# Softmax quotient of a dynamic convolution: sum in its own tile, limit on GpSimd, reciprocal in two separated halves

## The chip, the cores and the metric

The kernel runs on one core of a Trainium2 chip. All times are device microseconds of that core, from one launch. In profile lines PE is TensorE (PEld its weight loads), DVE is VectorE, ACT is ScalarE, POOL is GpSimd and SP is SyncE, which here only issues DMAs; a q behind a name is the engine's sequencer.

## The reference

The input is 8 images of 256 channels and 64 x 64 points, float32 throughout. Two residual layers follow each other. Layer 0 adds an involution: per point, 9 weights per group of 8 channels come out of a small network of 1 x 1 convolutions, and weigh a 3 x 3 neighbourhood. Layer 1 adds a local 7 x 7 attention and a dynamic convolution. The diff touches the second half of the dynamic convolution and the scaled weights of layer 0. Cut down to those:

```python
def _gn(v, G=32, eps=1e-5):                      # mean and variance of groups of 8 channels
    ...
    return ((g - m) / jnp.sqrt(s + eps)).reshape(v.shape)

x = x + _L0_conv_ref(_gn(x), ...)                # layer 0: x1, x2, x3 are 1x1 convolutions of _gn(x)
x = x + _L1_conv_ref(_gn(x), ...)                # layer 1

# inside layer 1, on y = _gn(x)
wts = jnp.einsum('oc,bchw->bohw', Wfc, y).reshape(b, C, 9, h, w)
wts = jax.nn.softmax(wts, axis=2)                # over the 9 branches of each channel
xr = jnp.broadcast_to(y[:, None], (b, 9, c, h, w)).reshape(b * 9, c, h, w)
hid = jax.nn.relu(_dwconv(xr, w1))
oc = _dwconv(hid, w2).reshape(b, 9, C, h, w)
out_conv = jnp.sum(oc * wts.transpose(0, 2, 1, 3, 4), axis=1)
return rate1 * out_att + rate2 * out_conv
```

The nine branches of `oc` are equal, so the kernel computes one depthwise result and multiplies it by the sum of the nine softmax weights, written out as a quotient. The middle branch's weights `Wfc` are subtracted from the other eight at the start, so that its exponential is 1. With T the sum of the eight other exponentials and S = min(1 + T, 1e37), the factor is S times the reciprocal of S.

## The kernel before, in words

**Tiling.** An image is cut into 8 bands of 8 rows; a band of one tile of 128 channels is 128 x 512 numbers. There are two channel tiles (`ct` 0 and 1). Layer 1 works through the 64 bands in order (`g` counts them), and a band takes 8 steps: four for `ct` 0 (`m` 0 to 3, steps 0 to 3) and four for `ct` 1 (steps 4 to 7). Layer 0 runs 12 bands ahead (`AHEAD`) and is woven into the same steps, so that the last image's layer 1 has no layer 0 beside it.

**A step of layer 1.** TensorE computes the attention's weighted values of an earlier step (L747) and the scores of this one (L703) into one PSUM tile `sco`. DVE masks the scores and takes their maximum (L712) and adds the weighted values to `xr` (L757). TensorE transposes the previous step's probabilities (L735). ACT takes the exponentials (L720), DVE the small reciprocal of their sums (L727, 128 x 2), ACT scales them (L729). Beside that, TensorE computes two of the eight branch products `pf` (L825, two matmuls each of them), ACT writes their exponentials into `ex` (L830, a tile of 128 x 2 x 512, three buffers), and POOL adds the tile of the step before into this one (L1026). DVE adds depthwise taps (L782, L808). One more group of matmuls may stand in the middle of a step: queries (L637), keys (L658), values (L563, L607).

**The order.** The kernel writes out each engine's order by hand. `after(n, f)` puts `f` at n places from now; `advance()` moves on by one place and runs what has come due. A step has six places: after the scores and L757; after the first `pf`; after L729; after the middle group; after the second `pf`; at the step's end. Every engine executes its instructions in the order in which this one program issued them.

**The quotient.** After a channel tile's last step, `dynamic_sum` comes four places later. It lets POOL add the two halves of the last `ex` tile (L838) into the second half. Five places later, at the next step's first place, DVE adds 1 and limits the sum (L845, `tensor_scalar`) and takes the reciprocal of the first half (L846, 256 columns); three places later it takes the other half's (L850); two places later POOL multiplies (L855), multiplies `oc` (L856) and adds into `xr` (L857). After the second channel tile, six places later, SP stores `xr` (L862). For the very last tile of the launch, DVE does POOL's part.

**Scaled weights.** Once per image, `scaled_weights` multiplies layer 0's weights by the group norm's factor, per input channel: L296 (128 x 64) and L297 (128 x 256), twice each, on DVE. The factor comes from `gn_affine`, whose last part takes a small reciprocal on DVE (L266).

**Layer 0's part in a step.** L328 and L369 are its 1 x 1 convolutions, L429 and L447 the small network, L460 (DVE) the product of the nine weights with shifted values into `prod` (two buffers), and L468 (POOL) adds `prod` into `xg`. The adds of one band stand in the order of its nine products.

Of the kernel before, what the change touches and what calls it, by code (L numbers as in the profile page):

```python
# [10 lines left out]
F32 = mybir.dt.float32  # L11
BF16 = mybir.dt.bfloat16
AF = mybir.ActivationFunctionType
ALU = mybir.AluOpType
# [4 lines left out]
P = 128  # L19
C = 256  # L20
NCT = C // P
# [3 lines left out]
BAND = R * W  # L25
# [61 lines left out]
def conv_layers_kernel(ctx: ExitStack, tc: tile.TileContext, ins: dict, out: bass.AP):  # L87
    nc = tc.nc
# [18 lines left out]
    def load(name, shape, src=None, now=True):  # L107
        t = const.tile(shape, F32, name=f"c_{name}")
        late.append(lambda: nc.scalar.dma_start(out=t, in_=ins[name] if src is None else src))
        if now:  # L110
            late.pop()()
        return t
# [5 lines left out]
    w12 = load("w12", [P, NCT, 2 * REL], ins["w12"].rearrange("(t p) n -> p t n", p=P))  # L118
    w3 = load("w3", [P, NCT, C], ins["w3"].rearrange("(t p) n -> p t n", p=P))
# [62 lines left out]
    w1 = ctx.enter_context(tc.tile_pool(name="l1", bufs=2))  # L182
# [3 lines left out]
    def layer1_loads():  # L186


        last = w1.tile([P, NCT, 1, C], F32, tag="rec", name="last", bufs=1)
        for f in late:  # L190
            f()
        nc.scalar.dma_start(out=last, in_=wfc_in[:, :, KK - 1 :])

        def first():
            nc.vector.tensor_scalar(wv, wv, rate1, None, ALU.mult)

        def difference(kt):
            nc.vector.tensor_sub(wfc[:, kt], wfc[:, kt], last[:, kt].to_broadcast([P, KK - 1, C]))  # L200

        return [first, lambda: difference(0), lambda: difference(1)]
# [12 lines left out]
    def after(n, f):  # L215
        later.append((place[0] + n, f))
# [8 lines left out]
    def gn_affine(sts, means, name, done):  # L225


        n = len(sts)
        mv = stat.tile([P, n, 2], F32, name=f"mv_{name}", tag=f"mv{n}")
        for ct, st in enumerate(sts):  # L230
            nc.vector.bn_aggr(mv[:, ct, :], st)
        mean, var = mv[:, :, 0], mv[:, :, 1]
        gm, d, sc, bi = (stat.tile([P, n], F32, name=f"{v}_{name}", tag=f"{v}{n}") for v in ("gm", "d", "sc", "bi"))

        def group_means(v, k):
            pg = ps.tile([P, n], F32, name=f"pg_{name}_{k}", tag="gen", bufs=5)
            nc.tensor.matmul(pg, means, v, start=True, stop=True)
            return pg


        def a1():
            pg = group_means(mean, 0)
            after(2, lambda: a2(pg))

        def a2(pg):
            nc.vector.tensor_copy(gm, pg)
            for ct in range(n):
                c = slice(ct, ct + 1)
                nc.vector.tensor_scalar(d[:, c], pg[:, c], mean[:, c], None, ALU.subtract)
                nc.vector.tensor_scalar(d[:, c], d[:, c], d[:, c], var[:, c], ALU.mult, ALU.add)  # L250
            after(5, a3)

        def a3():
            pg = group_means(d, 1)
            after(2, lambda: a4(pg))

        def a4(pg):
            nc.vector.tensor_scalar(sc, pg, GN_EPS, None, ALU.add)
            after(2, a5)

        def a5():
            nc.scalar.activation(sc, sc, AF.Sqrt)
            after(4, a6)

        def a6():
            nc.vector.reciprocal(sc, sc)  # L266
            for ct in range(n):
                c = slice(ct, ct + 1)
                nc.vector.tensor_scalar(bi[:, c], gm[:, c], sc[:, c], -1.0, ALU.mult, ALU.mult)
            done(sc, bi)  # L270

        after(3, a1)
# [15 lines left out]
    def scaled_weights(b):  # L288

        im = images[b]  # L290

        def scale(sc, bi):
            im.w12s = w0.tile([P, NCT, 2 * REL], F32, tag="w12s", name=f"w12s_{b}", bufs=1)
            im.w3s = w0.tile([P, NCT, C], F32, tag="w3s", name=f"w3s_{b}", bufs=1)
            for kt in range(NCT):
                nc.vector.tensor_scalar(im.w12s[:, kt], w12[:, kt], sc[:, kt : kt + 1], None, ALU.mult)  # L296
                nc.vector.tensor_scalar(im.w3s[:, kt], w3[:, kt], sc[:, kt : kt + 1], None, ALU.mult)  # L297
            after(5, lambda: through(bi))

        def through(bi):  # L300
            pb = ps.tile([P, 1 + NCT], F32, tag="gen", name=f"pb_{b}", bufs=5)
            for m, to, w in ((0, 0, w12), (0, 64, w12), (1, 0, w3[:, :, :P]), (2, 0, w3[:, :, P:])):
                for kt in range(NCT):
                    nc.tensor.matmul(
                        pb[to : to + w.shape[2], m : m + 1], w[:, kt], bi[:, kt : kt + 1],
                        start=(kt == 0), stop=(kt == NCT - 1),
                    )
            after(2, lambda: biases(pb))

        def biases(pb):  # L310
            im.bias = w0.tile([P, 1 + NCT], F32, tag="bias", name=f"bias_{b}")
            nc.vector.tensor_add(im.bias[:, 0:1], pb[:, 0:1], par[:, PB21 : PB21 + 1])
            for ct in range(NCT):
                nc.vector.tensor_add(
                    im.bias[:, 1 + ct : 2 + ct], pb[:, 1 + ct : 2 + ct], chan[:, ct, CB3 : CB3 + 1]
                )

        gn_affine([im.st0[:, ct] for ct in range(NCT)], gmat, f"a{b}", scale)

    def small_maps(b, i):  # L320
# [396 lines left out]
    def exponentials(nm, prob, nmax):  # L717
        tot = w1.tile([P, 2], F32, tag="tot", name=f"tot_{nm}", bufs=4)
        for h in range(2):
            nc.scalar.activation(  # L720
                prob[:, h, :NKEY], prob[:, h, :NKEY], AF.Exp, bias=nmax[:, h : h + 1], scale=-1.0,
                accum_out=tot[:, h : h + 1],
            )
        return tot
# [90 lines left out]
    def depthwise_end(b, i, ct, acc):  # L815

        oc = w1.tile([P, BAND], F32, tag="oc", name=f"oc_{b}_{i}_{ct}")
        nc.scalar.activation(oc, acc.rearrange("p r c -> p (r c)"), AF.Copy, scale=rate2)
        return oc
# [11 lines left out]

    def dynamic_sum(b, i, ct, ex, oc):

        tot = ex[:, 1]
        xr = images[b].xr[i]

        engine = nc.vector if (b, i, ct) == (B - 1, NB - 1, NCT - 1) else nc.gpsimd
        engine.tensor_add(tot, tot, ex[:, 0])  # L838
        rec = w1.tile([P, BAND], F32, tag="rec", name=f"rec_{b}_{i}_{ct}", bufs=1)
        n = BAND // 2  # L840

        def quotient():


            nc.vector.tensor_scalar(tot, tot, 1.0, 1.0e37, ALU.add, ALU.min)  # L845
            nc.vector.reciprocal(rec[:, :n], tot[:, :n])  # L846
            after(3, second)

        def second():
            nc.vector.reciprocal(rec[:, n:], tot[:, n:])  # L850
            after(2, weigh)

        def weigh():

            engine.tensor_mul(tot, tot, rec)  # L855
            engine.tensor_mul(oc, oc, tot)  # L856
            engine.tensor_add(xr[:, ct], xr[:, ct], oc)  # L857
            if ct == NCT - 1:
                after(6, store)

        def store():
            nc.sync.dma_start(  # L862
                out=out[b].rearrange("(t p) n -> p t n", p=P)[:, :, i * BAND : (i + 1) * BAND], in_=xr
            )

        after(5, quotient)


    def beside(g, s):
# [93 lines left out]
    with tc.manual_schedule():  # L963
# [17 lines left out]
        for n, f in enumerate(layer1_loads()):  # L981
            after(4 * STEPS * (3 + n), f)

        pending, before, conv = [], None, None
        for g in range(-AHEAD, B * NB):
            b, i = divmod(g, NB)
            for s in range(STEPS):
                ct, m = divmod(s, NT // 2)
                mid, end = beside(g, s)
                steer(g, s)  # L990
                if g >= 0:
# [9 lines left out]
                    tot = exponentials(nm, prob, nmax)  # L1001
                advance()
                if g >= 0:
                    ex, exb = w1.tile([P, 2, BAND], F32, tag="ex", name=f"ex_{nm}", bufs=3), ex if m else None
# [18 lines left out]
                if g >= 0:  # L1023
                    branch_weights(b, i, ct, m, 1, ex)
                    if exb is not None:
                        after(4, lambda ex=ex, exb=exb: nc.gpsimd.tensor_add(ex, ex, exb))  # L1026
                    if m == 1:
                        conv[1]()
                        conv = depthwise_middle(b, i, ct)
                    if m == NT // 2 - 1:  # L1030
                        oc = depthwise_end(b, i, ct, conv[1])
                        after(4, lambda a=(b, i, ct, ex, oc): dynamic_sum(*a))
# [97 lines left out]
```

## Time and profile before

| | |
|---|---|
| median of 3 runs | 4155.27 us (4154.16 to 4160.41) |
| the profiled execution | 4152.64 us |
| its span, first to last instruction | 4150.9 us |
| mean granted TensorE clock | 0.993 |
| busy PE, PEld | 4022.6 us (97%), 2126.8 us (51%) |
| busy DVE, ACT, POOL | 3591.9 us (87%), 3081.0 us (74%), 2923.0 us (70%) |
| L845 on DVE | 128 times, 136.9 us, and 33.0 us idle ahead of it |
| L846, L850 on DVE | 128 times each, 224.4 us and 223.5 us |
| L838, L855, L856, L857 on POOL | 127 times each, 161.5 to 162.3 us each |
| L296 and L297 on DVE | 16 times each, 15.9 us and 17.0 us |

A group's line gives, behind its shapes and its count, the busy time and the mean of one in ns, and then the idle time of the engine just before it with what ended that. Matmuls overlap in the records, so a PE that reads 97% busy can hide gaps of a tenth of a microsecond; a step's length against the matmuls in it shows them. The chain is followed back from the last instruction, from each to what released it.

### The profile page before, as it was taken

Reading aid. Unit: us, or ns where it says so; the run is one execution under the profiler, and the core shown is the slowest. Engines: PE = TensorE matmul, PEld = TensorE weight load, DVE = VectorE, ACT = ScalarE, POOL = GpSimd, SP = SyncE. Lnnn points to the kernel's source line nnn. Section 1 sums busy time; section 2 is a strip of 40 time slices with the busy share of each in tenths; the row PEclk is TensorE's granted clock in tenths of the full one; section 3 lists DMA queues with packets and bytes.
Section 4 is the critical chain, followed back from the end, with each engine's and each line's share of the span. In section 5 each row is a group of like instructions: output and inputs, shape, how many; then the busy total and the mean of one; then the engine's idle time right before and its main releaser. Section 6 shows DMA issues by size and latency. Waiting matters only on the chain.

```text
span 4150.9 us, 72735 instructions
## 1 busy us (share of the span) xinstructions
PE 4022.6 (97%) x25292; PEld 2126.8 (51%) x25292; DVE 3591.9 (87%) x7248; ACT 3081.0 (74%) x7726; POOL 2923.0 (70%) x1902
## 2 busy tenths in 40 slices
PE   6789999999999999999999999999999999999998
PEld 3345555555555555555555555555555555455554
DVE  5878998899898898889998898888988889977777
ACT  3467778777787777877778777777778777687776
POOL 4767777677786777777777777777777677744554
PEclk8999999999999999999999999999999999999999
DMA  8854234234244233334234234244233233111100
GB/s 226 194 135 111 73 91 109 72 94 109 62 101 107 76 94 98 81 94 109 72 85 118 72 94 105 66 101 106 71 82 99 65 87 85 33 41 39 39 28 21
DMA packets 381264, 367.89 MB, mean 89 GB/s; under 512 B 55648, under 2 KB 282720, under 8 KB 380640
## 3 DMA queue, kind: packets, MB, share of 16 engines
q1 hardware_dynamic: 377568, 358.68, 34.3%
q8 instruction: 200, 3.28, 0.3%
q10 hardware_dynamic: 3328, 4.55, 0.3%
q14 instruction: 168, 1.38, 0.1%
HBM read 261.42 MB, written 101.71 MB: 87 GB/s over the span
## 4 chain that ended last, share of the span: by engine, by line
PE 71%; DVE 14%; POOL 6%; ACT 5%; DMA 2%; issue 2%; SPq 1%; POOLq 0%; ACTq 0%; DVEq 0%
PE pf L825 33%; PE ptp L735 5%; PE sco L747 5%; PE pk L658 5%; PE sco L703 5%; PE p L369 5%; DVE prod L460 4%; PE pq L637 4%; POOL xg L468 3%; PE pvt L607 2%; PE pv L563 2%; DVE acc L808 2%; PE pw L447 2%; DVE acc L782 2%; POOL ex L1026 2%
## 5 line engine op out<-in xcount | busy, mean ns | idle before, releaser
L825 PE MATMUL pf<-yp,c_wfc 128*128 128x512 f32 x4096 | 1930.5, 595 | 10.6 <-ACT vc L581 5.0
L468 POOL TENSOR_TENSOR xg<-xg,prod 128x1024 f32<-128x1024 f32 x549 | 1203.9, 2193 | 96.6 <-DVE prod L460 64.1
L825 PEld LDWEIGHTS pf<-yp,c_wfc 128*128 128x128 f32 x4096 | 729.9, 190 | 690.5 <-issue 619.4
L1026 POOL TENSOR_TENSOR ex<-ex,ex 128x1024 f32<-128x1024 f32 x384 | 907.7, 2364 | 61.9 <-ACT ex L830 57.2
L830 ACT ACTIVATE ex<-pf 128x512 f32<-128x512 f32 x1024 | 607.3, 593 | 297.9 <-POOL ex L1026 141.3
L782 DVE SCALAR_TENSOR_TENSOR acc<-yp,c_chan,acc 128x504 f32<-128x504 f32 (+3 forms) x1104 | 766.2, 694 | 42.3 <-ACT acc L773 21.7
L460 DVE SCALAR_TENSOR_TENSOR prod<-pw,c_par,x3q 128x1040 f32<-128x1040 f32 x576 | 733.9, 1281 | 66.8 <-PE pw L447 21.6
L808 DVE SCALAR_TENSOR_TENSOR acc<-hid,c_chan,acc 128x504 f32<-128x504 f32 (+3 forms) x1024 | 757.8, 740 | 20.2 <-ACT acc L802 2.1
L855 POOL TENSOR_TENSOR ex<-ex,rec 128x512 f32<-128x512 f32 x127 | 162.3, 1278 | 809.5 <-DVE rec L850 767.1
L729 ACT ACTIVATE prob<-prob,tot 128x196 f32<-128x196 f32 x1024 | 411.6, 450 | 387.2 <-DVE tot L727 386.4
L712 DVE CUSTOM_DVE_ANT_0 prob<-sco,c_mask 128x196 f32<-128x196 f32 x1024 | 325.5, 355 | 272.4 <-PE sco L703 272.0
L720 ACT ACTIVATE prob<-prob,nmax 128x196 f32<-128x196 f32 x1024 | 461.4, 454 | 46.9 <-DVE nmax L712 45.3
L747 PEld LDWEIGHTS sco<-pt,vt 112*64 112x64 f32 x8160 | 283.8, 137 | 182.3 <-issue 51.7
L737 ACT COPY pt<-ptp 112x512 f32<-112x512 f32 x511 | 297.0, 581 | 105.0 <-PE ptp L735 103.0
L735 PE MATMUL ptp<-ident,prob 128*112 128x128 f32 x2044 | 341.7, 287 | 31.2 <-ACT prob L729 30.5
L747 PE MATMUL sco<-pt,vt 112*64 112x64 f32 x8160 | 347.0, 227 | 0.0
L735 PEld LDWEIGHTS ptp<-ident,prob 128*112 128x112 f32 x2044 | 203.9, 133 | 201.4 <-issue 77.7
L703 PE MATMUL sco<-kb,qb 64*64 64x196 f32 x4096 | 295.2, 357 | 0.0
L563 PE MATMUL pv<-yp,c_wv 128*128 128x512 f32 (+2 forms) x576 | 247.3, 554 | 0.6
L369 PE MATMUL p<-xc,w3s 128*128 128x512 f32 x512 | 244.4, 601 | 0.0
L658 PE MATMUL pk<-yp,c_wk 128*128 128x512 f32 (+2 forms) x576 | 240.8, 545 | 0.0
L637 PE MATMUL pq<-yp,c_wq 128*128 128x512 f32 x512 | 240.6, 592 | 0.0
(140 smaller groups left out, 5294.0 us busy)
## 6 DMA issues: line engine op xcount, KB each, us to landing
x<-x3n SPq DMA_DIRECT2D x128, 264.0 KB, 2.1
x3q<-x SPq DMA_DIRECT2D x128, 264.0 KB, 7.2
xc<-in_x SPq DMA_DIRECT2D x64, 512.0 KB, 5.0
xg<-in_x SPq DMA_DIRECT2D x256, 128.0 KB, 4.8
x<-xg SPq DMA_DIRECT2D x256, 128.0 KB, 2.4
yp<-x SPq DMA_DIRECT2D x128, 256.0 KB, 3.3
xr<-x SPq DMA_DIRECT2D x64, 512.0 KB, 5.8
out_x<-xr SPq DMA_DIRECT2D x64, 512.0 KB, 3.1
```

The lines of the kernel that those rows point to most:

```text
L369: nc.tensor.matmul(p3, im.w3s[:, kt, mt * P : (mt + 1) * P], im.xc[i][:, kt, :], start=(kt == 0), stop=(kt == NCT - 1),)
L460: nc.vector.scalar_tensor_tensor(prod[:, :, :RUN], pw[:, j, :RUN].unsqueeze(1).to_broadcast([P, SHARE, RUN]), par[:, PCB2 + k : PCB2 + k + 1],
L468: nc.gpsimd.tensor_add(im.xg[i], im.xg[i], rows(prod))
L703: nc.tensor.matmul(sco[half[t], h, :NKEY], qb[half[h], 2 * m + t].rearrange("p r c -> p (r c)"), kb[half[h], :, c0 : c0 + KW], start=True, ...
L720: nc.scalar.activation(prob[:, h, :NKEY], prob[:, h, :NKEY], AF.Exp, bias=nmax[:, h : h + 1], scale=-1.0, accum_out=tot[:, h : h + 1],)
L735: nc.tensor.transpose(ptp[:, h, ch], prob[:, h, ch * CHUNK : (ch + 1) * CHUNK], ident)
L747: nc.tensor.matmul(po[half[h], :, t * TQ : (t + 1) * TQ], im.vt[i + ch, m][:n, t, (2 * ct + h) * HD : (2 * ct + h + 1) * HD], pt[:n, h, ch ...
L782: nc.vector.scalar_tensor_tensor(o, yp[:, ct, ra + dr : rb + dr, ca + dc : cb + dc], chan[:, ct, CW1 + k : CW1 + k + 1], o, ALU.mult, ALU.add,
L808: nc.vector.scalar_tensor_tensor(o, hid[:, ra + dr : rb + dr, ca + dc : cb + dc], chan[:, ct, CW2 + k : CW2 + k + 1], o, ALU.mult, ALU.add,)
L825: nc.tensor.matmul(pf, wfc[:, kt, 2 * m + j, ct * P : (ct + 1) * P], images[b].yp[i][:, kt, PAD : PAD + R], start=(kt == 0), stop=(kt == N ...
L830: nc.scalar.activation(ex[:, j].rearrange("p (r c) -> p r c", r=R), pf, AF.Exp)
L1026: after(4, lambda ex=ex, exb=exb: nc.gpsimd.tensor_add(ex, ex, exb))
```

## The change

The sum of the exponentials gets a tile of its own, `tot`, instead of the second half of `ex`. Adding 1 and the limit move from DVE to POOL, directly behind the sum. The reciprocal's tile `rec` shrinks to 256 columns and is used for one half after the other: reciprocal on DVE, multiplication by POOL one place later. The halves come 7 and 11 places after the sum (before: 5 and 8), which is behind the small reciprocal L727 of the next step and at the first place of the step after that. The multiplication of `oc` and the addition into `xr` come 13 places after the sum (before: 10), and the store moves with them. The scaled weights go from DVE to ACT. The weights tile `last` of the start, which shared buffers with `rec`, now shares them with `oc`.

```diff
@@ layer1_loads
-        last = w1.tile([P, NCT, 1, C], F32, tag="rec", name="last", bufs=1)
+        last = w1.tile([P, NCT, 1, C], F32, tag="oc", name="last")
@@ scaled_weights
-                nc.vector.tensor_scalar(im.w12s[:, kt], w12[:, kt], sc[:, kt : kt + 1], None, ALU.mult)
-                nc.vector.tensor_scalar(im.w3s[:, kt], w3[:, kt], sc[:, kt : kt + 1], None, ALU.mult)
+                nc.scalar.activation(im.w12s[:, kt], w12[:, kt], AF.Copy, scale=sc[:, kt : kt + 1])
+                nc.scalar.activation(im.w3s[:, kt], w3[:, kt], AF.Copy, scale=sc[:, kt : kt + 1])
@@ dynamic_sum
-        tot = ex[:, 1]
+        tot = w1.tile([P, BAND], F32, tag="tots", name=f"tot_{b}_{i}_{ct}", bufs=1)
         xr = images[b].xr[i]
 
         engine = nc.vector if (b, i, ct) == (B - 1, NB - 1, NCT - 1) else nc.gpsimd
-        engine.tensor_add(tot, tot, ex[:, 0])
-        rec = w1.tile([P, BAND], F32, tag="rec", name=f"rec_{b}_{i}_{ct}", bufs=1)
-        n = BAND // 2
-
-        def quotient():
-
-
-            nc.vector.tensor_scalar(tot, tot, 1.0, 1.0e37, ALU.add, ALU.min)
-            nc.vector.reciprocal(rec[:, :n], tot[:, :n])
-            after(3, second)
-
-        def second():
-            nc.vector.reciprocal(rec[:, n:], tot[:, n:])
-            after(2, weigh)
+        engine.tensor_add(tot, ex[:, 1], ex[:, 0])
+
+
+        engine.tensor_scalar(tot, tot, 1.0, 1.0e37, ALU.add, ALU.min)
+        rec = w1.tile([P, BAND // 2], F32, tag="rec", name=f"rec_{b}_{i}_{ct}", bufs=1)
+
+        def quotient(u):
+            v = tot[:, u * BAND // 2 : (u + 1) * BAND // 2]
+            nc.vector.reciprocal(rec, v)
+            after(1, lambda: engine.tensor_mul(v, v, rec))
 
         def weigh():
 
-            engine.tensor_mul(tot, tot, rec)
             engine.tensor_mul(oc, oc, tot)
             engine.tensor_add(xr[:, ct], xr[:, ct], oc)
...
-        after(5, quotient)
+        after(7, lambda: quotient(0))
+        after(11, lambda: quotient(1))
+        after(13, weigh)
```

## The prediction

> **What bounds the kernel now.** I read the page first, then the chain of waits, then stretches of the timeline.
>
> ```profile
> PE 4022.6 (97%) x25292; PEld 2126.8 (51%) x25292; DVE 3591.9 (87%) x7248; ACT 3081.0 (74%) x7726; POOL 2923.0 (70%) x1902
> ...
> PE 71%; DVE 14%; POOL 6%; ACT 5%; DMA 2%; issue 2%; SPq 1%; POOLq 0%; ACTq 0%; DVEq 0%
> ```
>
> TensorE bounds it; only where the chain leaves TensorE can anything be won. The chain of the second image (747 to 1246 us) leaves it at one place in nearly every band: around the first channel tile's quotient, in steps 5 to 7. Here it is in the band from 816.3 to 877.9 us (start, length, what):
>
> ```profile
> 852.03 2.33 POOL ex L1026
> ...
> 854.43 1.28 POOL ex L838
> ...
> 855.73 2.40 DVE ex L845
> ...
> 858.15 1.75 DVE rec L846
> ...
> 861.27 0.08 DVE tot L727
> ...
> 861.37 0.47 ACT prob L729
> ...
> 861.88 0.78 PE ptp L735 x4
> ```
>
> POOL's sum comes late, DVE then spends 2.40 + 1.75 us on the quotient, the small reciprocal L727 comes behind that, ACT waits for it, and TensorE waits for ACT. The view of L845 alone (shortest, median and longest in ns) shows why 2.40:
>
> ```profile
> L845 DVE TENSOR_SCALAR ex<-ex x128: 408/418/2858, 295.6 to 4141.0; 128x512 f32<-128x512 f32 x128
> ```
>
> It needs 0.42 us alone, but up to 2.86: the long ones lie on a POOL instruction (at 855.73 on an L468 from 855.66 to 857.84). The groups, by shape, give the prices:
>
> ```profile
> L845 DVE TENSOR_SCALAR ex<-ex 128x512 f32<-128x512 f32 x128 | 136.9, 1070 | 33.0 <-POOL ex L838 32.9
> ...
> L633 POOL COPY kb<-kb 128x420 f32<-128x420 f32 x112 | 60.1, 536 | 0.0
> ...
> L297 DVE TENSOR_SCALAR w3s<-c_w,sc_a 128x256 f32<-128x256 f32 x16 | 17.0, 1060 | 0.0
> ```
>
> How much TensorE loses I took from the timeline: a step's length (from L703 to the next L703) less the matmuls in it, by the chain's lengths (1.72 us for four 512-column ones, 0.62 + 0.51 + 0.58 for L747, L703, L735 and so on). The second image's eight bands lose 3.4, 1.2, 1.2, 3.1, 1.2, 1.7, 0.8 and 1.7 us, 14.3 of 499. The last image loses next to nothing (380 us from 3720: PE 379.15). With six full images and half a seventh some 90 us can be won at most.
>
> POOL matters too. From 831.97 (L855, after 5.95 us idle for L850) to 855.70 (the end of L838) its instructions follow without a gap: it sets when the next sum is ready.
>
> **What the Trainium skill says.** "SBUF — State Buffer", section "Who interferes with whom": DVE's `tensor_scalar` may use two ports, then shares a pair with GpSimd, and the later of the two blocks for the other's whole instruction. The trace agrees: 408 ns to 2858 ns for one shape. "GPSIMD Engine Reference", section "Engine selection": one-input operations run at about line rate there, two-input ones at half of VectorE's; agreed for the copy L633 (420 columns, 536 ns) against L838 (512 columns, 1272 ns). "ScalarE: Activation LUTs", section "What ACT_TABLE_LOAD costs": 280 ns + 0.833 ns per column with a pointer operand, so 443 ns at 196 columns; L729 takes 450.
>
> **The change, part by part.**
>
> *Off DVE:* L845, 128 x 1070 ns = 137 us, with its 33 us of waiting; L296 and L297, 15.9 + 17.0 = 33 us. The reciprocals (224 us each) stay.
>
> *Onto POOL:* the limit. No row shows it. Copies of 64 columns (L357, 234 ns) and 420 (536) give 0.85 ns per column, so 0.6 us at 512; the two-input sum gives 1.27 as the other end; below nothing it can't be, since POOL gets an instruction more. I take **0.7 us** (one input, two operations). Two half multiplications replace one: L838 (1272 ns at 512) and L468 (2193 at 1024) give 1.8 ns per column, so 0.81 each, +0.34. 127 x 1.04 = 132 us more on POOL, 70% to 74%.
>
> *Onto ACT:* 0.33 and 0.49 us, twice per image (that page's price), 1.6 us; nothing and 3.3 us are its ends. ACT now waits for L266; L737 and L720 stand behind it, and TensorE behind them. In band 3 L720 would start at about 979.2 instead of 978.0, and its L727 is due at 980.6 instead of 986.44: covered.
>
> *Moved:* before, L845 and L846 stood ahead of the step's L727. Now the first half stands behind it, and the second half (1.75 us) ahead of the next step's L727. POOL's L856 and L857 move behind L468 twice and L1026. The `ex` tile comes free with the sum, so that ACT's wait for L856 (24.5 us in all) goes. SP's store goes out at about 844.5 instead of 835.98 in this band; SP's loads behind it move too, and SP is idle from 845.5 to 877.9, which hides 8.5 us. `last` needs its buffer in the start alone: nothing.
>
> *A band, step 0 at 816.3, worked through.* The first product still waits for TensorE's L447 (at 830.4), so lands at 831.8, and L468 starts at once (before: 835.91). The second product is behind the second reciprocal: scores at 832.1, L712 and L757 to 833.0, 1.75, then 1.2: 836.0. L468 to 838.2, L1026 840.6, half multiplication, copy, L856 and L857 844.5, L468 and L1026 849.1, two L468 853.5, L1026 855.9, sum 857.2, limit **858.0**, 2.3 us behind L838's old end. DVE has done L727 at 857.0 (before: 861.3), so waits about 1 us there, with the urgent work done. It ends the half at 859.8, taps, product 862.5, L712 and L757 863.3, second half 865.1, product and taps 867.7, L727 at 867.8 against 869.1. Both stalls go: 1.2 us. The same sum over the other bands: band 0, DVE gains its 1.21 + 2.38 us, 2.6 of 2.7 us go (its other 0.7 lies at the image's start); band 3, 2.8 of 3.1 (L296 and L297, 4.6 us there from 977.55 to 982.14, are gone from DVE); band 5, 1.5 of 1.7; band 6, nothing (a table load, L262, on ACT).
>
> *Band 7 goes the other way.* Its steps are short and POOL is behind: L838 ended at 1224.72. Now the weighing no longer fits in ahead of the first product (TensorE gives it at 1202.75): 1204.0 for L468, second product 1207.8, then as above; the sum ends at 1228.5, the limit at **1229.3**. DVE has done its L727 at 1225.4 and waits almost 4 us. Its backlog runs through the chain to the next image's start, and the next L727 comes at 1238.8 instead of 1236.84. Counted from TensorE's product at the band's start, the image ends **2.0 us** later than before: the 2.4 us lost there (1.7, and 0.7 in the next band 0) become 4.4.
>
> *Sum per image:* 2.6 + 3 x 1.2 + 2.8 + 1.5 - 2.0 = 8.5 us. Six images 51, the seventh's first bands 5; the last tile on DVE has one multiplication more, 0.2. **56 us off** the profiled execution's 4152.64 (its span of 4150.9 and 1.7 around it): 4096.6. The median of the runs shown lies 2.6 above that execution, so I forecast **4099**.
>
> **The rivals.**
>
> A, full gain: POOL, no longer idle for the whole reciprocal (767 us over L855), keeps up in band 7 too. For it: its load is 74%. Against: the continuous POOL chain above. 90 us less: about 4065.
>
> B, a small gain or none: the bands with 1.2 us have a few tenths of room, and the half ahead of L727 takes it. Every 0.1 us more on POOL between product and limit costs a tenth in seven bands of each image, 45 us per us over the launch. At a limit of 56 / 45 + 0.7 = 1.9 us nothing is left: 4147 to 4163.
>
> C, slower: GpSimd does the limit at a per-column price like DVE's reciprocal (1753 ns for 256, 6.8 ns), 3.5 us. Beyond 1.9 us it costs 45 per us, (3.5 - 1.9) x 45 = 72: about 4227. For it: no row shows the operation. Against: the copies.
>
> D: the sum and the limit don't reach DVE's queue any earlier because every engine hands over twice more (reciprocal, multiplication, reciprocal in one small tile). The second half needs the first multiplication: POOL needs L468, L621 and 0.8, 4.2 us after the limit, DVE 5.3. With 0.6 to 1 us of room it holds; if not, it falls in with B.
>
> **How the numbers follow.** A measurement can tell 0.2% here, 8 us. My own case has 0.50, A 0.10, a gain smaller than mine but over 8 us 0.15, no change 0.08, C and other losses 0.17. The own case with 0.6 to 1.27 us for the limit reaches from 4070 to 4125. The range goes from A's 4064 to no change, 4156.
>
> **What would show it.** Right: no `tensor_scalar` of 512 columns on DVE; the limit on POOL at 0.6 to 0.8 us; ACT's wait for L727 (386.4 us) down by half; L855's wait (767 us) replaced by shorter ones at the half multiplications; L830's waits for POOL (141.3 and 24.5) lower; bands 1 and 2 at 60.4 us instead of 61.6; a new wait of DVE's first half for POOL, longest in band 7. Wrong: a limit over 1.3 us, POOL over 80%, or band 7 and the next band 0 longer by several us.

## The result, and the profile after

The median after is **4146.84 us** (4142.36 to 4151.57, 20 runs), before 4155.55 us (4152.74 to 4160.41, 20 runs): ratio 0.9979, 95% interval 0.9972 to 0.9986. The change gains 9 us, where 56 were forecast. It lies inside the range of the forecast, near its slow end.

The page after, engines and chain:

```profile
PE 4025.7 (97%) x25292; PEld 2134.1 (51%) x25292; DVE 3414.6 (82%) x7090; ACT 3092.9 (75%) x7758; POOL 3170.8 (76%) x2156
...
PE 44%; POOL 21%; DVE 19%; ACT 7%; issue 5%; DMA 2%; SPq 2%; POOLq 0%; DVEq 0%; ACTq 0%
```

VectorE (DVE) lost 177 us of work and GpSimd (POOL) gained 248, where the forecast said 132. TensorE's share of the chain fell from 71% to 44%: the work that sets the end now runs through POOL and DVE in more places. That share is no time. The span is 6 us shorter all the same, because the chain can follow another engine through stretches in which TensorE is busy too.

The groups by shape, for the limit (L841), the reciprocals (L846), POOL's additions of the layer 0 products (L468), and ACT's scaling behind the small reciprocal (L729). Behind the count: busy time, mean of one in ns, and the idle time ahead of it with what ended that:

```profile
L468 POOL TENSOR_TENSOR xg<-xg,prod 128x1024 f32<-128x1024 f32 x549 | 1200.8, 2187 | 377.6 <-DVE prod L460 357.6 <-DVE sc_a L258 3.5 <-DVE gm_b L246 3.2
...
L846 DVE RECIPROCAL rec<-tot 128x256 f32<-128x256 f32 x256 | 446.1, 1742 | 123.7 <-POOL tot L841 123.7
L729 ACT ACTIVATE prob<-prob,tot 128x196 f32<-128x196 f32 x1024 | 411.9, 452 | 356.1 <-DVE tot L727 356.0
...
L841 POOL TENSOR_SCALAR tot<-tot 128x512 f32<-128x512 f32 x127 | 243.6, 1918 | 11.1
```

and two of the same groups before:

```profile
L468 POOL TENSOR_TENSOR xg<-xg,prod 128x1024 f32<-128x1024 f32 x549 | 1203.9, 2193 | 96.6 <-DVE prod L460 64.1 <-DMA xc<-in_x 6.2 <-DVE sc_a L258 4.1
...
L729 ACT ACTIVATE prob<-prob,tot 128x196 f32<-128x196 f32 x1024 | 411.6, 450 | 387.2 <-DVE tot L727 386.4
```

The limit takes **1.92 us**, not 0.7. DVE waits 123.7 us for it. ACT's wait for L727 stands at 356.0 us (386.4 before), not at half. L468 waits 357.6 us for DVE's products (64.1 before): POOL now idles ahead of them and works after them.

I cut the second image into its bands (from L703 to L703 eight steps on), in us:

| band | 0 | 1 | 2 | 3 | 4 | 5 | 6 | 7 | sum |
|---|---|---|---|---|---|---|---|---|---|
| before | 68.8 | 61.6 | 61.6 | 63.9 | 61.6 | 62.1 | 59.3 | 60.0 | 498.7 |
| after | 67.3 | 61.2 | 61.2 | 62.5 | 61.2 | 61.2 | 59.5 | **64.25** | 498.2 |

Six bands win 0.4 to 1.5 us (0.4 in bands 1, 2 and 4, where 1.2 was forecast), band 6 loses 0.2 and band 7 loses 4.3. Only the seventh image, whose last bands have no layer 0 beside them, wins more: 475.8 to 469.5 us. That is 6.4 of the 9 us; the six full images together win 2.6. Band 7 of the second image in the chain of waits (start, length, what):

```profile
1224.74 1.28 POOL tot L838
1226.10 1.93 POOL tot L841
1228.06 1.75 DVE rec L846
...
1237.27 0.81 ACT prob L729 x2
...
1239.88 0.86 PE sco L703 x8
1240.74 1.03 PE ptp L735 x4
...
1248.34 0.51 PE sco L703 x8
1248.85 0.58 PE ptp L735 x4
```

Sum, limit and first half (L846) follow each other without a gap. Through DVE's work behind them (two products, the second half, taps) the chain comes to L729 and at last to TensorE's transposes (L735).

A second loss follows there. TensorE has nothing to do for 2.42 us (1236.19 to 1238.61), and from 1239.8 to 1243.2 us its granted clock (the share of full speed that it is allowed) reads 0.50, with 1.00 on both sides: L703 takes 0.86 us in that stretch and 0.51 later, L735 1.03 and 0.58. In the kernel after, such a stretch of 3.4 us (called half clock from here on) stands in band 7 of each of the first six images; the kernel before and e1 (below) have none there. Its price shows in two kernels of the experiments in which some images have it in band 7 and others don't: 63.6 us against 62.0 in e7, 63.9 against 62.3 in e4. So about 1.6 of band 7's 4.3 us are the clock's, some 10 us over the launch (an estimate from these numbers and the six stretches). In e7 and e4 TensorE's idle time ahead of it is the same in the bands with and without the stretch (1.8 and 2.0 us), so what else decides it stays open.

POOL's timeline shows why the sum is late there; ahead of the brackets start, length and instruction, in them idle time and what ended it. The kernel before:

```profile
1201.46 1.27 POOL L855 TENSOR_TENSOR ex<-ex,rec 128x512 f32<-128x512 f32 x1 [5.01 <-DVE rec L850]
...
1204.17 1.28 POOL L857 TENSOR_TENSOR xr<-xr,oc 128x512 f32<-128x512 f32 x1
1205.41 4.44 POOL L468 TENSOR_TENSOR xg<-xg,prod 128x1024 f32<-128x1024 f32 x2
...
1223.45 1.27 POOL L838 TENSOR_TENSOR ex<-ex 128x512 f32<-128x512 f32 x1
```

and the kernel after, in the same view and the same stretch of the band:

```profile
1201.90 2.18 POOL L468 TENSOR_TENSOR xg<-xg,prod 128x1024 f32<-128x1024 f32 x1 [2.66 <-DVE prod L460]
1205.57 2.17 POOL L468 TENSOR_TENSOR xg<-xg,prod 128x1024 f32<-128x1024 f32 x1 [1.48 <-DVE prod L460]
...
1210.02 0.74 POOL L847 TENSOR_TENSOR tot<-tot,rec 128x256 f32<-128x256 f32 x1
...
1212.19 1.29 POOL L852 TENSOR_TENSOR xr<-xr,oc 128x512 f32<-128x512 f32 x1
...
1224.74 1.27 POOL L838 TENSOR_TENSOR tot<-ex 128x512 f32<-128x512 f32 x1
1226.10 1.92 POOL L841 TENSOR_SCALAR tot<-tot 128x512 f32<-128x512 f32 x1
```

Before, the weighing (three times 1.28 us) covered POOL's wait for the first product (DVE ended it at 1203.94), and from the first L468 to the sum it took 18.0 us (1205.41 to 1223.45). After, POOL idles 2.66 and 1.48 us for the two products, and then does 0.74 + 1.27 + 1.29 us of the weighing behind them: 22.8 us (1201.90 to 1224.74), and 1.92 for the limit on top.

### The profile page after: what moved, and what is told of

Same layout as the page of the kernel before. It is cut to its first block, busy times and chain, and to the rows that moved or that the text cites. A ratio compares the mean times of both kernels' runs of the same rounds, so it can differ in the third digit from the quotient of the medians.

```text
span 4144.8 us, 72568 instructions
## 1 busy us (share of the span) xinstructions
PE 4025.7 (97%) x25292; PEld 2134.1 (51%) x25292; DVE 3414.6 (82%) x7090; ACT 3092.9 (75%) x7758; POOL 3170.8 (76%) x2156
## 4 chain that ended last, share of the span: by engine, by line
PE 44%; POOL 21%; DVE 19%; ACT 7%; issue 5%; DMA 2%; SPq 2%; POOLq 0%; DVEq 0%; ACTq 0%
PE pf L825 20%; POOL xg L468 9%; DVE rec L846 6%; POOL ex L1023 5%; DVE prod L460 5%; PE sco L747 3%; PE pk L658 3%; PE ptp L735 3%; PE sco L703 3%; PE p L369 2%; PE pq L637 2%; DVE acc L782 2%; DVE acc L808 2%; POOL tot L841 2%; PE pvt L607 2%
## 5 line engine op out<-in xcount | busy, mean ns | idle before, releaser
L468 POOL TENSOR_TENSOR xg<-xg,prod 128x1024 f32<-128x1024 f32 x549 | 1200.8, 2187 | 377.6 <-DVE prod L460 357.6
L808 DVE SCALAR_TENSOR_TENSOR acc<-hid,c_chan,acc 128x504 f32<-128x504 f32 (+3 forms) x1024 | 756.7, 739 | 18.1
L830 ACT ACTIVATE ex<-pf 128x512 f32<-128x512 f32 x1024 | 604.1, 590 | 207.3 <-PE pf L825 192.4
L729 ACT ACTIVATE prob<-prob,tot 128x196 f32<-128x196 f32 x1024 | 411.9, 452 | 356.1 <-DVE tot L727 356.0
L846 DVE RECIPROCAL rec<-tot 128x256 f32<-128x256 f32 x256 | 446.1, 1742 | 123.7 <-POOL tot L841 123.7
L847 POOL TENSOR_TENSOR tot<-tot,rec 128x256 f32<-128x256 f32 x254 | 185.5, 730 | 326.6 <-DVE rec L846 326.6
L735 PE MATMUL ptp<-ident,prob 128*112 128x128 f32 x2044 | 339.8, 288 | 6.7 <-ACT prob L729 5.8
L703 PE MATMUL sco<-kb,qb 64*64 64x196 f32 x4096 | 296.7, 359 | 0.0
L735 PEld LDWEIGHTS ptp<-ident,prob 128*112 128x112 f32 x2044 | 206.6, 134 | 169.4 <-issue 94.9
L841 POOL TENSOR_SCALAR tot<-tot 128x512 f32<-128x512 f32 x127 | 243.6, 1918 | 11.1
```

The costliest lines, as they stand in the source:

```text
L468: nc.gpsimd.tensor_add(im.xg[i], im.xg[i], rows(prod))
L703: nc.tensor.matmul(sco[half[t], h, :NKEY], qb[half[h], 2 * m + t].rearrange("p r c -> p (r c)"), kb[half[h], :, c0 : c0 + KW], start=True, ...
L735: nc.tensor.transpose(ptp[:, h, ch], prob[:, h, ch * CHUNK : (ch + 1) * CHUNK], ident)
L808: nc.vector.scalar_tensor_tensor(o, hid[:, ra + dr : rb + dr, ca + dc : cb + dc], chan[:, ct, CW2 + k : CW2 + k + 1], o, ALU.mult, ALU.add,)
L830: nc.scalar.activation(ex[:, j].rearrange("p (r c) -> p r c", r=R), pf, AF.Exp)
L846: nc.vector.reciprocal(rec, v)
```

## The experiments

Each kernel is named by its label. The kernel before ran beside each set on the same chip, at medians of 4153.7 to 4157.4 us; differences below 4 us between sets are not read. L numbers shift by a few lines where an edit adds some. The theories of the first set are P (only the price of the limit was wrong) and Q (the new order eats the gain).

### The price of the limit, all else as after

`e1_copy` and `e2_none` leave out adding 1 and the limit; the first puts a copy in the place.

```diff
-        engine.tensor_scalar(tot, tot, 1.0, 1.0e37, ALU.add, ALU.min)
+        engine.tensor_copy(tot, tot)                       # e1_copy; e2_none: nothing
+        engine.tensor_scalar(tot, tot, 1.0, None, ALU.add)    # e3_twice: two of one
+        engine.tensor_scalar(tot, tot, 1.0e37, None, ALU.min) # operation each
```

> The changed kernel with POOL's limit replaced by a copy of the sum onto itself on POOL (128 x 512, one input); adding 1 and the limit are left out. The copy should take 0.6 us, about the price that the prediction took for the limit (0.7), where the limit itself took 1.92. Theory P (the price of the limit alone was wrong): the forecast gain comes back, 55 to 65 us against the kernel before, about 4095, and band 7 of the second image, now 64.25 us, falls to about 62. Theory Q (the new order of halves and weighing eats the gain, whatever the limit costs): 4130 to 4147, bands 1 and 2 stay at 61.2.

> The changed kernel without the limit on POOL at all (adding 1 and the limit are left out). Theory P, with 45 us per us of the limit: some 25 us less than with the copy, about 4070, unless the 90 us that can be won at most are reached first. Theory Q: 4125 to 4147, hardly less than the changed kernel's 4147.

> The changed kernel with POOL adding 1 and limiting in two instructions of one operation each. Measures what one operation costs there. If a GpSimd tensor_scalar costs by the instruction (1.9 us each), POOL pays 3.8 us and theory P expects 1.9 x 45 = 85 us more than now, about 4230; if it costs by the operation (0.96 each), no change. Theory Q expects no more than the changed kernel plus 20 us in either case.

| POOL between sum and first half | us of POOL | median | ratio to before |
|---|---|---|---|
| e2_none: nothing | 0 | 4095.7 | 0.9861 (0.9846 to 0.9876) |
| e1_copy: copy | 0.61 | 4103.1 | 0.9881 (0.9864 to 0.9897) |
| after: limit | 1.92 | 4146.8 | 0.9979 (0.9972 to 0.9986) |
| e3_twice: two instructions | 2.98 | 4218.0 | 1.0155 (1.014 to 1.017) |

The groups by shape of e1_copy:

```profile
L846 DVE RECIPROCAL rec<-tot 128x256 f32<-128x256 f32 x256 | 445.8, 1741 | 55.7 <-POOL tot L841 55.6
...
L841 POOL COPY tot<-tot 128x512 f32<-128x512 f32 x127 | 77.4, 609 | 8.1
```

and of e3_twice:

```profile
L841 POOL TENSOR_SCALAR tot<-tot 128x512 f32<-128x512 f32 x127 | 189.6, 1493 | 11.1
L842 POOL TENSOR_SCALAR tot<-tot 128x512 f32<-128x512 f32 x127 | 189.1, 1489 | 10.5
```

At 0.61 us the kernel takes 4103, four more than forecast. A `tensor_scalar` of one operation takes 1.49 us, of two 1.92, a copy 0.61. From row to row that is about 12, then 33, then 67 us per us of POOL: each step further finds more bands without slack. In the second image only band 7 grows from e2 to e1 (60.7 to 61.3), from e1 to the limit bands 1, 2, 4 and 5 grow as well (60.4 to 61.2), and in e3 all eight. The half clock adds to it: with the first 20 us of the first image left out, the profiled execution of e1 has none of these stretches in the first seven images, the kernel after six, e3 sixteen. At 1.6 us each that is about 10 of the 44 us from e1 to the limit and 16 of the 71 us from there to e3 (estimate).

### The order, with the limit on DVE

```diff
@@ dynamic_sum, e4_dve_limit, against after
-        engine.tensor_scalar(tot, tot, 1.0, 1.0e37, ALU.add, ALU.min)
...
         def quotient(u):
+            if u == 0:
+                nc.vector.tensor_scalar(tot, tot, 1.0, 1.0e37, ALU.add, ALU.min)
```

> The changed kernel with the limit back on DVE, directly ahead of the first half's reciprocal (behind the small reciprocal). POOL is rid of 1.92 us per channel tile, DVE pays 0.42 us alone and up to 2.6 where POOL's next add starts at the same moment. Theory P: the first half comes no earlier than now in the bands whose sum comes late (2.4 us on DVE in place of 1.9 on POOL), but POOL runs 1.9 us further ahead for all that follows, so band 7 loses less: 4105 to 4135. Theory Q: no change, 4140 to 4150.

4181.4 us, ratio 1.0069 (1.0054 to 1.0084): slower than before, where P had said 4105 to 4135. Its group by shape (idle time behind the last stroke):

```profile
L846 DVE TENSOR_SCALAR tot<-tot 128x512 f32<-128x512 f32 x128 | 145.7, 1139 | 41.6 <-POOL tot L838 41.6
```

The limit costs DVE 1.14 us (1.07 before), and the new places and weights on ACT don't pay for themselves: bands 1 and 2 take 62.0 us (61.6 before). P is not the whole answer, and the next set puts the limit into the old order.

### Parts of the change in the old order

```diff
@@ e5_old_order, against before; e6_old_order_copy has tensor_copy(tot, tot) there and so leaves out 1 and limit
         engine.tensor_add(tot, tot, ex[:, 0])
+        engine.tensor_scalar(tot, tot, 1.0, 1.0e37, ALU.add, ALU.min)
...
-            nc.vector.tensor_scalar(tot, tot, 1.0, 1.0e37, ALU.add, ALU.min)
             nc.vector.reciprocal(rec[:, :n], tot[:, :n])
@@ e8_weights_alone, against before (e9_old_order_weights: both edits)
-                nc.vector.tensor_scalar(im.w12s[:, kt], w12[:, kt], sc[:, kt : kt + 1], None, ALU.mult)
+                nc.scalar.activation(im.w12s[:, kt], w12[:, kt], AF.Copy, scale=sc[:, kt : kt + 1])
... 
```

> The kernel before with one edit: the limit goes to POOL, directly behind the sum, still in place in the second half of ex; order of the quotient and weights as before. Theory P (what counts is when the limited sum is there: price of the limit on POOL): in the band from 816.3 us the sum ends at 855.7, the limit at 857.65 instead of DVE's 858.13, so L846 starts about 0.4 us earlier at best, and POOL's work behind it comes 1.9 us later only where POOL did not wait for the reciprocal anyway: bands 1, 2 and 4 win 0 to 0.4 us, band 7 loses; 4135 to 4160. Theory R (the order of the halves behind L727 is what brings the gain): in the old order L846 stands ahead of L727 and makes it wait for POOL, so slower than before: 4160 to 4200.

> As the run above, with a copy in place (0.61 us as measured) in place of the limit; adding 1 and the limit are left out. Theory P: the limited sum would be there at 856.3 instead of 858.13, 1.8 us earlier, which is more than the 1.2 us that the band loses: about as good as the new order with the copy, 4100 to 4115. Theory R: the old order keeps L846 ahead of L727, and most of the loss stays: 4125 to 4150, bands 1, 2 and 4 at 61 us or more.

> The kernel before with only the scaled weights (L296, L297) on ACT. The prediction's step: L296 and L297 hold DVE 4.6 us in band 3 of an image, so band 3 wins 1.3 to 2.8 us (63.9 to 61.1 to 62.6): 4136 to 4147. Rival (band 3's gain in the kernel after comes from the quotient alone, or ACT loses as much as DVE wins): 4150 to 4160, band 3 at 63.5 or more.

> The kernel after with the quotient in the order of before: limit on POOL behind the sum, weights on ACT, and then L846, L850 and the whole weighing at the places 5, 8 and 10, in the second half of ex and a rec of 512. Against the kernel after it differs in the order and the tiles of the quotient alone. Theory O (new order puts the weighing between the products and the sum, where POOL has no slack, and in the old order POOL did it while it waited for the product): 4120 to 4131, which is 16 to 27 us faster than the kernel after. Rival (the order is worth nothing and the 4129.7 of the old order came from the weights staying on DVE): 4140 to 4150.

| sum comes by | old places (5, 8, 10) | new places (7, 11, 13) |
|---|---|---|
| copy on POOL, 0.61 us | e6: 4097.2 | e1: 4103.1 |
| limit on POOL, 1.92 us | e5: 4129.7; e9: 4129.8 | after: 4146.8 |
| limit on DVE | e8: 4147.1 | e4: 4181.4 |

The weights are on ACT in e8, e9 and the right column. In every row the new places are slower, by 6, 17 and 34 us, so theory R (the new order brings the gain) is out in this table: it had 4160 to 4200 for e5 and 4125 to 4150 for e6. P's values are missed too, on the good side. In e9 only the order and the tiles of the quotient differ from the kernel after (ratios to before 0.9936, 0.9923 to 0.9948, and 0.9979); of the 17 us about 8 are half clock (one stretch in e9, six in the kernel after; estimate). Moving the limit gains by itself, 27 us (e5: 0.9937, 0.9925 to 0.995), half of the forecast even at 1.92 us, and more than the 0 to 0.4 us per band that I had worked out: bands 1 and 2 go from 61.6 to 60.9. The weights alone gain 9 us (0.9977, 0.9967 to 0.9986), in the second image all of it in band 3 (63.9 to 62.3); once the limit is off DVE they gain nothing, since band 3 is at 62.3 already (e5).

### Which of the moved pieces costs

```diff
@@ e12_old_places / e13_first_half_moved / e14_weighing_moved, against after
-        after(7, lambda: quotient(0))
-        after(11, lambda: quotient(1))
-        after(13, weigh)
+        after(5, ...); after(8, ...); after(10, weigh)     # e12
+        after(7, ...); after(8, ...); after(10, weigh)     # e13
+        after(5, ...); after(8, ...); after(13, weigh)     # e14
@@ e16_first_half_in_order, against e13
             after(1, lambda: engine.tensor_mul(v, v, rec))
+            if u == 0:
+                after(1, lambda: quotient(1))
...
-        after(8, lambda: quotient(1))
```

In e13 (and in e15 below) the second half is issued ahead of the first multiplication and overwrites the small `rec`, so that the first half is multiplied by the second half's reciprocals; DVE never waits for POOL there. e16 and e17 have that in order.

> The kernel after with its own tile tot and its small rec used twice, but the halves at 5 and 8 places behind the sum and the weighing at 10, as before (after: 7, 11, 13). Theory O (the places cost the time): 4115 to 4132. Rival (what costs is the hand-over through one small rec, since the second reciprocal must wait until POOL has multiplied the first half): 4138 to 4165, with a wait of L846 for L847 of 1 us and more in most bands.

> The kernel after with places 7, 8 and 10 for first half, second half and weighing (after: 7, 11, 13; old places: 5, 8, 10, which gave 4124.6). Theory S (the second half and the weighing behind the products cost the time, the first half behind L727 is good in itself, since DVE waits for POOL there with less behind it): 4100 to 4120, band 7 at 60 to 61 us, bands 1 and 2 at 60.4 to 60.6. Rival F (the first half's late place costs it): 4135 to 4147.

> The kernel after with places 5, 8 and 13: halves at the old places, only the multiplication of oc and the addition into xr late (2.6 us of POOL, behind both products instead of ahead of them). Theory S: slower than the 4124.6 of the old places: 4130 to 4147, most of it in band 7. Rival F: 4120 to 4128.

> As e13 (4120.5), but the second half is issued behind the first half's multiplication, at the same place 8, so that L846 of the second half waits until POOL has multiplied the first; the whole quotient is computed as in the kernel after. Theory S with a cheap hand-over: 4118 to 4128. Rival H (DVE waits for POOL at that hand-over, 0.7 us and what POOL has ahead of it, in every band): 4130 to 4150.

| kernel | places | median | ratio to before | bands 1 and 2 (second image) | band 7 |
|---|---|---|---|---|---|
| e12 | 5, 8, 10 | 4124.6 | 0.9921 (0.9908 to 0.9935) | 60.8, 60.8 | 60.3 |
| e14 | 5, 8, 13 | 4133.6 | 0.9946 (0.9934 to 0.9959) | 60.8, 60.8 | 61.7 |
| e13 | 7, 8, 10, no hand-over | 4120.5 | 0.9914 (0.99 to 0.9927) | 61.0, 61.1 | 60.7 |
| e16 | 7, 8, 10, in order | 4140.3 | 0.9964 (0.995 to 0.9978) | 61.3, 61.2 | 61.3 |
| after | 7, 11, 13 | 4146.8 | 0.9979 (0.9972 to 0.9986) | 61.2, 61.2 | 64.25 |

The multiplication of `oc` and the addition into `xr` behind the products cost 9 us (e14), in band 7 alone, as theory S had it. The first half behind L727 costs nothing by itself (e13 against e12). But the second half early behind it needs a hand-over: DVE may write `rec` again when POOL has multiplied, and rival H was right there, 20 us (e16 against e13). From e14 to the kernel after, which has both halves later too, 13 us more are lost; about 8 of them are half clock (one stretch against six; estimate), and no run moves the second half alone. e12 against e9 also prices the tiles, at the same places: the sum's own tile and the small `rec`, with its multiplication in two halves, win 5 us, and ACT waits for POOL at L830 for 96.1 instead of 170.5 us.

### The addition into xr later

```diff
@@ e7_late_add, against after (e10, e11, e15, e17, e18: likewise, 15 places behind weigh at 10)
             engine.tensor_mul(oc, oc, tot)
-            engine.tensor_add(xr[:, ct], xr[:, ct], oc)
-            if ct == NCT - 1:
-                after(6, store)
+            after(12, add)
+
+        def add():
+            engine.tensor_add(xr[:, ct], xr[:, ct], oc)
+            if ct == NCT - 1:
+                after(2, store)
```

> The kernel after with the limit on POOL; only L852, the addition into xr (1.27 us, nobody waits for it but the store), comes 12 places later, behind the next channel tile's sum and limit, and the store 2 places behind it. The amount of work on POOL stays the same. Theory P (the chain on POOL from product to limit): 1.27 + 0.06 us less ahead of every limit, as if the limit cost 0.6 instead of 1.92: 4100 to 4112, band 7 from 64.25 to 61.5 us or less. Rival (POOL's load as a whole sets the pace, wherever the addition stands): 4138 to 4150.

> The kernel before with the limit on POOL behind the sum and the addition into xr 15 places later than the weighing, behind the next channel tile's sum and limit; the store 2 places behind it. Weights on DVE, the order of the halves as before. If the chain from product to limit is what counts, 1.33 us go from it and the limit costs as much as the copy did in this order (4097.2): 4095 to 4106. Rival (POOL's whole load, which stays at 3155 us): 4125 to 4132.

> As the run above, with the weights on ACT. If the weights bring what they brought alone (9 us, band 3 from 63.9 to 62.3 us): 4086 to 4098. Rival (band 3's stall is gone already once DVE is rid of the limit, 62.27 us with the weights on DVE): no difference from the run above within 4 us.

> As e13, with the addition into xr 15 places behind the weighing and the store 2 places behind it: the limit stays on POOL, the weighing stands ahead of the products, and the chain to the limit is 1.33 us shorter. Theory S: bands 1, 2, 4 and 5 at 60.4 us, band 7 at 60.0 to 61.0; 4094 to 4112, about the forecast of 4099 and faster than both kernels. Rival F: 4115 or more.

> As e15 (4087.9), with the second half issued behind the first half's multiplication as in e16: the whole of the reference is computed, limit on POOL, weighing at place 10, addition into xr 15 places later. Theory S with a cheap hand-over: 4086 to 4098, faster than the kernels before and after. Rival H: 4105 to 4125.

> The tiles of the kernel before (sum in the second half of ex, rec of 512 columns), limit on POOL behind the sum, weights on ACT, first half at place 7, second at 8, the whole weighing at 10, addition into xr 15 places later, store 2 places behind it. No hand-over between the halves, so as e15 (4087.9): 4086 to 4100, faster than the kernels before and after. Rival T (the tile ex held until the weighing, which e15 did not have, makes ACT's L830 wait, as in the kernel before): 4105 to 4125.

| kernel, addition late | places | rec | median | ratio to before |
|---|---|---|---|---|
| e7 | 7, 11, 13 | 256 | 4120.8 | 0.9915 (0.9902 to 0.9929) |
| e10, weights on DVE | 5, 8, 10 | 512 | 4120.4 | 0.9913 (0.9899 to 0.9926) |
| e11 | 5, 8, 10 | 512 | 4121.3 | 0.9913 (0.99 to 0.9927) |
| e15, no hand-over | 7, 8, 10 | 256 | 4087.9 | 0.9837 (0.9824 to 0.9851) |
| e17, in order | 7, 8, 10 | 256 | 4166.2 | 1.0028 (1.0018 to 1.0038) |
| **e18** | 7, 8, 10 | 512 | **4090.1** | 0.9840 (0.9827 to 0.9853) |

e7 gains 26 us against the kernel after with POOL's work unchanged: the chain ahead of the sum counts, not POOL's load. I expected 4100 to 4112; bands 1 and 2 did reach 60.4 us, but band 7 only fell to 62.0 in the first image and, with the half clock, to 63.6 in the next five. With the addition late, the new places (e7) and the old ones (e11) take the same time. In the old order it gains 9 us instead of the 24 and more expected (e10): the quotient at place 5 stands ahead of L727, and bands 1 and 2 stop at 60.8.

For the hand-over, the waits of DVE's reciprocals for POOL (us in total, times, longest), in e16:

```profile
DVE rec L846 <- POOL tot L841: 75.6, 42, 2.5
...
DVE rec L846 <- POOL tot L847: 50.8, 48, 1.5
```

and in e17:

```profile
DVE rec L846 <- POOL tot L847: 112.9, 54, 2.8
...
DVE rec L846 <- POOL tot L841: 36.9, 42, 1.8
```

The wait for the limit halves with the late addition, and the wait for the multiplication (L847) doubles. In e17 POOL has the late addition, an L468 and L621 between the limit and that multiplication. In band 1 of the second image DVE's second half begins 46.2 us behind the band's start (e15: 44.6), the next L727 at 52.5 (50.8), and the band is 1.0 us longer. The whole second image takes 499.9 us for e15's 489.9, and the seven images together 77 of the 78 us that e17 loses against e15. Five of them also have a half-clock stretch in band 0 (70.8 us against 69.1). How the wait reaches TensorE I have followed in band 1 alone.

**e18** needs no hand-over: tiles of before, `rec` of 512 columns. It computes all of the reference and is 67 us faster than before (4157.4 beside it) and 57 us faster than the kernel after. Against e11 only the places 7 and 8 for 5 and 8 differ: the first half behind L727 is worth 31 us once the addition is out of the way. Its page:

```profile
PE 3999.0 (98%) x25292; PEld 2127.8 (52%) x25292; DVE 3416.2 (84%) x7089; ACT 3113.1 (76%) x7758; POOL 3151.8 (77%) x2029
...
PE 89%; DVE 3%; POOL 3%; ACT 2%; DMA 1%; issue 1%; SPq 1%; ACTq 0%; DVEq 0%; POOLq 0%
```

and its groups by shape:

```profile
L729 ACT ACTIVATE prob<-prob,tot 128x196 f32<-128x196 f32 x1024 | 411.2, 451 | 196.8 <-DVE tot L727 195.9
...
L735 PE MATMUL ptp<-ident,prob 128*112 128x128 f32 x2044 | 332.5, 285 | 0.2 <-ACT prob L729 0.2
...
L839 POOL TENSOR_SCALAR ex<-ex 128x512 f32<-128x512 f32 x127 | 243.8, 1920 | 11.1
...
L846 DVE RECIPROCAL rec<-ex 128x256 f32<-128x256 f32 x128 | 222.6, 1739 | 48.1 <-POOL ex L839 48.1
```

The limit still takes 1.92 us; ACT's wait for L727 is halved at last (195.9 us), TensorE's L735 waits 0.2 us for it, bands 1, 2, 4 and 5 are at 60.4 and band 7 at 60.0. POOL's timeline in its band 7:

```profile
1187.66 1.28 POOL L855 TENSOR_TENSOR ex<-ex,rec 128x512 f32<-128x512 f32 x1 [5.38 <-DVE rec L850]
...
1190.26 4.46 POOL L468 TENSOR_TENSOR xg<-xg,prod 128x1024 f32<-128x1024 f32 x2
...
1208.34 1.27 POOL L838 TENSOR_TENSOR ex<-ex 128x512 f32<-128x512 f32 x1
1209.69 1.92 POOL L839 TENSOR_SCALAR ex<-ex 128x512 f32<-128x512 f32 x1
```

The weighing is ahead of the products again, and the sum follows 18.1 us behind the first L468 (1190.26 to 1208.34).

## Why the prediction was wrong

- **The step that failed: the limit's price.** "I take 0.7 us (one input, two operations)", from copies on POOL. The row of a copy held for a copy (0.6 worked out, 0.61 measured) and not for an operation with a scalar. The upper bound of 1.27, the two-input sum, was no bound: one operation took 1.49 us and two 1.92. The measurement decides here also against the sentence of the Trainium skill that I leaned on ("GPSIMD Engine Reference", section "Engine selection": one-input operations at about line rate): at 512 columns the one-input `tensor_scalar` was slower than the two-input addition.
- **The sum held at the price it was made for, in part by luck.** With the copy's 0.61 us the same edit gives 4103.1, inside the case's own 4070 to 4125; but two errors cancel in it, since the full images win less and the seventh more than forecast (bands below). Rival B's working ("At a limit of 56 / 45 + 0.7 = 1.9 us nothing is left: 4147 to 4163") comes close: 4146.8 at 1.92. C was the same mechanism at a higher price. The slope, 45 us per us throughout, is 12 below 0.61, 33 up to 1.92 and 67 beyond, and the half clock that is part of the last two was in no term of the forecast.
- **What the gain was credited to was wrong.** I charged the new places 2.0 us per image in band 7 and credited "both stalls go" to the half behind L727. The old places were better in every row of the table with e4 to e9: with the copy they too bring bands 1 and 2 to 60.4 us (e6), so at that price the stalls go without the half behind L727. That half is worth 31 us with the addition late (e18 against e11) and 4 without (e13 against e12). At 1.92 us the places cost 17 us (e9) to 22 us (e12), and the limit's move brings 27 alone (e5). Band 7 was rightly named, and its mechanism (weighing behind the first product, DVE waiting "almost 4 us": 3.0 at the copy's price, 4.35 at the real one) was as told; its size, 2.0 us in the forecast, was 1.3 us at the copy's price and 4.3 at the real one, 1.6 of these from the half clock.
- **Bands at the copy's price,** before less e1: 1.2 in bands 1, 2 and 4 as forecast, 1.65 in band 5 (1.5), 1.6 in band 0 (2.6), 1.4 in band 3 (2.8), -0.2 in band 6 (0), -1.3 in band 7. 6.6 us per image for 8.5, and 12.3 in the seventh for 5.
- **The weights:** 338 and 496 ns on ACT (0.33 and 0.49 forecast, from "ScalarE: Activation LUTs", section "What ACT_TABLE_LOAD costs"; the runs agree). They were worth 9 us alone, and nothing beside the other edit; adding the two gains in band 3 was a double count.
- **Hand-overs (D)** do not bind in the kernel after, where the second half is four places later: its DVE waits for L841 alone. They bind as soon as the second half is moved up (e16).
- **Small terms:** the half multiplications take 0.73 us (0.81 forecast). ACT's waits for POOL at L830 fell from 141.3 and 24.5 to 11.7 us, as forecast.

## What to carry to other kernels

Price an operation from a row of its own kind on its own engine; where there is none, give the term a wide range, or settle it with one run of that instruction. On an engine that feeds others in a fixed order, work that nobody waits for belongs behind the piece that somebody waits for, and into the time in which the engine idles anyway; moving it past that idle time costs where the work behind has no slack (e14 moved 2.6 us: 1.4 us lost in band 7, nothing in bands 1 and 2). A smaller tile used twice is a hand-over between two engines, and its price shows only when the second use comes soon.

## What the runs showed of the hardware

- On GpSimd, 128 x 512 in float32: copy 0.61 us, two-input addition 1.27, `tensor_scalar` with one operation 1.49, with two 1.92. The second operation in the same instruction costs 0.43 us, in an instruction of its own 1.49.
- The same `tensor_scalar` on DVE takes 0.43 us alone (the launch's last tile, in the kernel after). Its means of 1.07 (before) and 1.14 us (e4) are mixtures: in the kernel before 80 of the 128 took 0.42 us on average and 48 took 2.16. All 48 began while GpSimd was executing an L468 or L621 and ended 0.3 to 0.8 us behind the end of that instruction. The Trainium skill ("SBUF — State Buffer", section "Who interferes with whom") says that such an instruction can take the port pair that DVE shares with GpSimd, and that the later of the two is then blocked for the other's whole instruction; the 48 agree.
- That is where e5's gain comes from in bands 1, 2 and 4. In the second image the limit took DVE 2.38 us there for the first channel tile; with it on GpSimd the first half begins 0.73 us earlier from the band's start (41.11 us in e5's band 1, 41.84 before), as much as the band wins. At 0.42 us DVE's limit would have let it begin 2 us earlier than it did (an estimate from these numbers), and GpSimd's 1.92 us would have been a loss. No run has the limit on DVE with GpSimd kept still, so for the whole launch the split of the 27 us stays open.
- TensorE's granted clock read 0.50 for stretches of 3.4 us, in the kernel after 1.1 to 1.5 us behind the end of TensorE's idle time of 2.4 us in band 7. One such stretch cost 1.6 us of a band (e4, e7). Idle times of equal length came with it and without it.
